# A GRU with a residual on one core: eight input units of the third step ahead of z's product in step 0, and one transfer moved

## Chip, cores and metric

The kernel runs on one core of a Trainium2 chip. The metric is the device time of one execution in microseconds (us). TensorE is called PE in the profile, its weight loads PEld; VectorE is DVE, ScalarE ACT, GpSimd POOL, and SP is the engine on whose queue most transfers are issued.

## What is computed

A GRU with 64 sequences, 128 steps, 512 inputs and 512 states, added to its own input. Every fourth step (but the last) the state goes through one more layer before the next step. Cut to what matters:

```
def step(h, inp):
    x_t, prop = inp
    comb = concatenate([x_t, h])
    z = sigmoid(comb @ Wz + bz)
    r = sigmoid(comb @ Wr + br)
    h_cand = tanh(concatenate([x_t, r * h]) @ Wh + bh)
    h_new = (1 - z) * h + z * h_cand
    h_next = where(prop, tanh(h_new @ Wp + bp), h_new)
    return h_next, h_new

return x + all h_new
```

All data are 32-bit floats. The upper 512 rows of each weight matrix meet x, the lower 512 the state.

## The kernel before

**Layout.** The 512 states stand as two halves (S = 2) of N = 256 columns, the 64 sequences of each half in 64 of the 128 partitions. A product over 512 rows has four blocks of 128 rows (k = 0 to 3, taken in ORDER = 0, 2, 1, 3). One *unit* is one block for one gate: `product` (L234) issues it for both halves, and the trace shows 4 matmuls of 128x256 for it (all on L225).

**State products and input products.** The weights for the state are in `wh[0..2]` (r, z, candidate), those for x in `wx`. A step needs the state products in order: r, then z, then the candidate with r * h. The input products don't depend on the state. They are kept as a list of units in `queue`; `fill(n)` (L416) issues the next n of them, so that they stand between the state products and give PE work while the other engines compute. When the last unit of a list has gone, `read_out()` (L423) issues the copies that bring its result, with the bias, from PSUM to the tile `cp` (L435 for r and z, L440 for the candidate; DVE). For steps 0 to 3 the units are plain (`plain`, L427: 12 units a step; for the third step in the order r, z, candidate, for the fourth block by block). From the fifth step on four steps at a time go through fewer products at the price of sums of weights and inputs (`batch`); the sums of weights are made once, in the first steps: `sum_outer` (L319 to L321, DVE, into the tiles `tw`), `sum_outer_1` (L325, DVE, in place), `sum_inner` and `sum_inner_1` (L328 to L330, L333, on POOL, a few on DVE).

**Order.** The schedule is written by hand: each engine runs its instructions in the order of the program text. PE, DVE, ACT and POOL each go through theirs one by one, with semaphores between the engines.

**Transposes.** A product takes its left operand transposed. `turn` (L241) does this for one half of the columns: four PE transposes (L248) and a copy out of PSUM (L239) by DVE or ACT. `turn_x(t)` turns x of step t (8 transposes, 2 copies), which the plain units of that step need. From the fifth step on x arrives by another route: small transfers `xs` (L157) and DVE transposes (`join_x`, L281).

**Step 0**, in the order of the text: r's four units (L728), then `turn_x(2)` (L732); r's sigmoid (L751) and rh = r * h (L752); three units of z (L762), rh's transposes (L766), z's fourth unit (L770); z and 1 - z (L775, L776), keep = (1 - z) * h (L777, DVE); `sum_outer` (L789) and `sum_inner` of one product (L791, POOL); `fill(12)` (L797), which are the 12 plain units of the third step; `turn_x(3)` (L799); the candidate's four units; then the copies of the third step's result, the tanh (L808, ACT), its product with z (L809) and the sum with keep (L814), both DVE, once for each half of the columns; `fill(5)` of the fourth step's units, the transposes of the new h's first half, one unit, those of its second half, six units; then `sum_outer_1` and `sum_inner_1` on DVE, and the first transposes of the `xs` route.

**Transfers at the start.** They are issued on SP one after the other: x of the first two steps, the weights for x (r, z, candidate), the weights for the state r, then x of the third and fourth step in two transfers, the weights for the state z and the candidate, sixteen `xs` transfers, the weights of the additional layer, its bias, and x of the next four steps.

Of the kernel before, what the change touches and what calls it, by code (L numbers as in the profile page):

```python
# [17 lines left out]
def kernel(  # L18
# [41 lines left out]
    R, Z, H_ = range(3)  # L60
# [32 lines left out]
    def load_x(tile_, t0, n, j=0):  # L93
        for s in range(S):
            nc.sync.dma_start(
                out=tile_[s * B : (s + 1) * B, j : j + n, :], in_=x[:, t0 : t0 + n, ts(s, N)]
            )

    def load_w(wt, w, k0, k1, eng):
        eng.dma_start(  # L100
            out=wt[:, k0:k1, :],
            in_=w[k0 * P : k1 * P, :].rearrange("(k p) n -> p k n", p=P),
        )

    ORDER = [s * C + c for c in range(C) for s in range(S)]
    xr = {}
# [33 lines left out]
    for i in range(3):  # L140
        for k in (0, 2):
            load_w(wh[i], gates_in[i][D:, :], k, k + 2, nc.sync)
        if i == 0:
            load_x(xr[0], 2, 2, 2)

    dummy = const.tile([1, 1], F32, name="dummy")
    nc.scalar.activation(dummy, ones[:, 0:1], AF.Sigmoid)
# [74 lines left out]
    def products(ps, lhs, rhs, start=False):  # L222

        for s in range(S):
            nc.tensor.matmul(  # L225
                ps[s * B : (s + 1) * B],
                lhsT=lhs,
                rhs=rhs(s),
                start=start,
                stop=True,  # L230
                skip_group_check=True,
            )

    def product(ps, lT, w, k, start=False):  # L234
        s0, c0 = divmod(k, C)
        products(ps, lT[:, c0, ts(s0, B)], lambda s: w[:, k, ts(s, N)], start)
# [4 lines left out]
    def turn(src, dst, c, name, eng):  # L241


        pt = turn_ps[c][:, :P].bitcast(BF16).rearrange("p (w n) -> p w n", w=2)
        for s in range(S):
            words = src[:, c * P + s * B : c * P + (s + 1) * B].bitcast(BF16)
            for w in range(2):
                nc.tensor.transpose(  # L248
                    pt[s * B : (s + 1) * B, w, :],
                    words.rearrange("p (n w) -> p w n", w=2)[:, w, :],  # L250
                    ident16,
                )
        copy(
            eng,
            dst[:, c, :].bitcast(U16).rearrange("p (n w) -> p n w", w=2),
            pt.bitcast(U16).rearrange("p w n -> p n w"),
        )
# [7 lines left out]
    def new_xT(g):  # L265
        if g not in xT:
            xT[g] = xtp.tile([P, Q4, C, P], F32, tag="xT", name=f"xT_{g}")

    def turn_x(t, eng=nc.scalar):
        g, i = divmod(t, Q4)  # L270
        new_xT(g)
        src = xr[g]
        for c in range(C):
            turn(src[:, i, :], xT[g][:, i], c, f"xT_{t}", eng)
# [141 lines left out]
    def fill(n):  # L416
        for _ in range(min(n, len(queue))):
            unit, end = queue.pop(0)
            unit()
            if end is not None:  # L420
                pending.append(end)
# [5 lines left out]
    def plain(t):  # L427

        first, second = scratch[:2] if t % 2 == 0 else scratch[2:]
        regions = (first[:, :N], first[:, N:], second[:, :N])  # L430
        g, i = divmod(t, Q4)

        def end():
            new_cp(t // 2)
            nc.vector.tensor_add(  # L435
                G[t][:, :, 0:2, :],
                first.rearrange("p (g c n) -> p c g n", g=2, c=C),
                bias[:, :, 0:2, :],
            )
            nc.vector.tensor_add(G[t][:, :, 2, :], cut(second[:, :N]), bias[:, :, 2, :])  # L440


        order = [(e, k) for e in range(3) for k in ORDER]
        if t == Q4 - 1:
            order = [(e, k) for k in ORDER for e in range(3)]
        units = [
            lambda e=e, k=k: product(
                regions[e], xT[g][:, i], wx[:, :, e, :], k, k == ORDER[0] and e != Z
            )
            for e, k in order  # L450
        ]
        return [(u, None) for u in units[:-1]] + [(units[-1], end)]
# [113 lines left out]
    def batches(g):  # L566

        if g * Q4 >= T:
            return []
        ms = [(g, i) for i in (1, 2, 6, 5, 7, 3, 4)]  # L570
        if g + 1 < LAST:
            ms += [(g + 1, i) for i in (1, 6, 2, 5, 3, 7, 4)]
        return sum((batch((g, n), ms[2 * n : 2 * n + 2]) for n in range(7) if 2 * n < len(ms)), [])
# [103 lines left out]
    for t in range(T):  # L677
# [6 lines left out]
        places = PLACES[u]  # L684
        if t == 0:
            queue.extend(plain(2) + plain(3))
            places = (12, 12)
        elif t == 1:
            queue.extend(batch((1, 0), [(1, 1), (1, 2)]))
            places = (8, 6)  # L690
        elif t == 2:
            queue.extend(batch((1, 1), [(1, 10), (1, 11)]) + batch((1, 2), [(1, 8), (1, 9)]))
            places = (12, 8)
        elif t == 3:
            queue.extend(batches(FIRST))
            places = (8, 8, 6)
        elif u == 7:

            queue.extend(batches(even + 2))
        thin = t >= T - 9  # L700
        if thin:

            places, behind = TAIL[t - (T - 9)]
        if t == T - 10:
# [7 lines left out]
            places = (4, 5)  # L712
# [13 lines left out]


        for k in ORDER:  # L728
            product(slots[R], hT, wh[R], k)
        if t < 2:  # L730
            if t == 0:
                turn_x(2)  # L732
        if t == 1:
            for i in (5, 7):
                sum_inner(i, nc.gpsimd)
# [19 lines left out]
            seed(H_, t)  # L755
        join(0)

        if t in (2, 3):
            fill((16, 6)[t - 2])


        for k in ORDER[: 2 if thin else 3]:  # L762
# [194 lines left out]
```

## Time and profile before

| | us |
|---|---|
| median of 3 runs | 1329.04 |
| their range | 1328.59 to 1329.49 |
| the profiled execution | 1330.24 |
| its span, first to last instruction | 1328.5 |
| PE busy (share) | 1319.2 (99%) |
| DVE, ACT, POOL busy | 750.8, 554.4, 881.5 |
| mean granted clock of PE | 0.999 |
| start of z's product, step 0 | 22.78 |
| start of the candidate's product, step 0 | 31.18 |

How to read it: a timeline line has the start from the beginning of the span, the time from the first start to the last end of the merged instructions, the engine, the source line, the operation, what it writes and reads, how many, and in brackets how long the engine stood before it and what ended that. Matmuls overlap: 16 of them start 1.73 us apart from the next group although the line gives 1.90 us, so durations of PE are taken from start to start.

### The profile page before, as it was taken

What the parts mean: (1) busy time and instruction counts of PE and PEld (TensorE: products, weight loads), DVE (VectorE), ACT (ScalarE), POOL (GpSimd) and SP (SyncE); (2) the same over time, 40 slices, a digit from 0 to 9 for tenths busy, and PEclk for the clock granted to TensorE, in tenths of its full rate; (3) what the DMA queues carried; (4) which work ended last, traced back from release to release, by engine and by line L of the source; (5) the groups of instructions that cost most, each with busy time, mean ns of one, the idle gap of its engine ahead of it and who ended that gap; (6) DMA issues with size and microseconds to landing.
All of it is one profiled execution on the core that took longest, in us unless ns stands there. A gap on an engine that the chain in (4) does not pass through costs nothing.

```text
span 1328.5 us, 37727 instructions
## 1 busy us (share of the span) xinstructions
PE 1319.2 (99%) x15312; PEld 1117.0 (84%) x15312; DVE 750.8 (57%) x2000; ACT 554.4 (42%) x1733; POOL 881.5 (66%) x1032
## 2 busy tenths in 40 slices
PE   9999999999999999999999999999999999999998
PEld 5888888888888888888888888888888888888865
DVE  3655555555555555555555555555555555555544
ACT  1344444444444444444444444444444444444433
POOL 4876766766767577675777757676676676757530
PEclk9999999999999999999999999999999999999999
DMA  8421122121121221222111221212212112121030
GB/s 236 90 50 30 21 49 49 33 49 34 33 49 33 54 45 18 49 43 56 33 33 34 50 49 34 47 20 49 49 34 49 34 33 49 33 49 33 18 104 17
DMA packets 171438, 62.22 MB, mean 47 GB/s; under 512 B 133600, under 2 KB 166496, under 8 KB 171264
## 3 DMA queue, kind: packets, MB, share of 16 engines
q1 hardware_dynamic: 170880, 59.47, 20.8%
q8 instruction: 121, 1.98, 0.6%
q14 instruction: 53, 0.43, 0.1%
q10 hardware_dynamic: 224, 0.20, 0.1%
q0 software_dynamic: 160, 0.14, 0.0%
HBM read 43.00 MB, written 16.78 MB: 45 GB/s over the span
## 4 chain that ended last, share of the span: by engine, by line
PE 96%; SPq 1%; DMA 1%; DVE 0%; issue 0%; ACT 0%; DVEq 0%; ACTq 0%
PE rc L225 33%; PE zp L225 20%; PE scratch_q L225 11%; PE scratch_r L225 11%; PE scratch_x L225 11%; PE scratch_a L225 5%; PE turn L248 5%; DMA xr<-in_x_dram 1%; SPq L157 1%; SPq L100 0%; DMA bias<-in_L_cond_bp_dram 0%; DVE wx L333 0%; DVE turn L809 0%; SPq L115 0%; DVE xT L281 0%
## 5 line engine op out<-in xcount | busy, mean ns | idle before, releaser
L225 PE MATMUL rc<-wh,rhT 128*64 128x256 f32 x2048 | 246.0, 379 | 0.0
L580 POOL TENSOR_TENSOR cp<-mb,mb 128x768 f32<-128x768 f32 x75 | 136.3, 1818 | 107.4 <-ACT rc L410 47.5
L225 PE MATMUL zp<-wh,hT 128*64 128x256 f32 x1536 | 204.6, 379 | 0.0
L225 PEld LDWEIGHTS rc<-wh,rhT 128*64 128x64 f32 x2048 | 168.6, 137 | 40.1
L225 PE MATMUL rc<-wh,hT 128*64 128x256 f32 x1536 | 186.5, 383 | 0.4
L891 POOL TENSOR_TENSOR xr<-xr,h 128x256 f32<-128x256 f32 x127 | 92.7, 730 | 126.3 <-DVE h L814 126.3
L225 PEld LDWEIGHTS rc<-wh,hT 128*64 128x64 f32 x1536 | 122.3, 137 | 36.1 <-issue 10.1
L580 POOL TENSOR_TENSOR cp<-mb 128x768 f32<-128x768 f32 x47 | 85.3, 1815 | 94.7 <-DVE h L814 89.8
L225 PEld LDWEIGHTS zp<-wh,hT 128*64 128x64 f32 x1536 | 119.7, 137 | 24.7
L809 DVE TENSOR_TENSOR turn<-turn,z 128x128 f32<-128x128 f32 x256 | 75.4, 295 | 102.2 <-ACT turn L808 100.7
L239 DVE COPY rhT<-turn 128x256 uint16<-128x256 uint16 x256 | 97.6, 420 | 56.0 <-PE turn L248 51.6
L751 ACT ACTIVATE turn<-rc 128x128 f32<-128x128 f32 x256 | 55.3, 260 | 171.4 <-issue 113.8
L239 ACT COPY hT<-turn 128x256 uint16<-128x256 uint16 x127 | 47.3, 373 | 165.5 <-DVE hT L239 130.7
L548 DVE TENSOR_TENSOR mb<-scratch_r,cq 128x384 f32<-128x384 f32 (+1 forms) x107 | 59.3, 554 | 91.8 <-ACT cq L547 90.3
L580 POOL TENSOR_TENSOR mb<-mb,mb 128x768 f32<-128x768 f32 x58 | 105.4, 1817 | 8.5 <-DVE mb L550 8.5
L541 DVE TENSOR_TENSOR cx<-scratch_r,cx 128x384 f32<-128x384 f32 (+1 forms) x107 | 59.3, 554 | 88.0 <-ACT cx L539 88.0
L775 ACT ACTIVATE z<-zp 128x256 f32<-128x256 f32 x128 | 49.2, 384 | 136.7 <-PE zp L225 136.7
L410 ACT COPY rc<-cp 128x256 f32<-128x256 f32 x256 | 96.4, 377 | 18.3 <-DVE cp L435 4.6
L808 ACT ACTIVATE turn<-rc 128x128 f32<-128x128 f32 x256 | 55.2, 260 | 112.8 <-PE rc L225 111.7
L814 DVE TENSOR_TENSOR h<-turn,keep 128x128 f32<-128x128 f32 x254 | 74.1, 292 | 15.2
L248 PEld LDWEIGHTS <-h 128*64 128x64 bf16 x1016 | 68.1, 110 | 12.2 <-DVE h L814 6.5
L248 PE MATMUL turn<-ident,h 128*64 128x128 bf16 x1016 | 77.8, 220 | 0.3 <-DVE h L814 0.3
(165 smaller groups left out, 2931.7 us busy)
## 6 DMA issues: line engine op xcount, KB each, us to landing
xs<-in_x_dram SPq DMA_DIRECT2D x248, 64.0 KB, 2.8
xr<-in_x_dram SPq DMA_DIRECT2D x62, 256.0 KB, 4.1
out_dram<-xr SPq DMA_DIRECT2D x62, 256.0 KB, 3.3
wx<-in_L_cond_Wr_dram SPq DMA_DIRECT2D x7, 256.0 KB, 4.5
wx<-in_L_cond_Wz_dram SPq DMA_DIRECT2D x2, 512.0 KB, 6.4
wx<-in_L_cond_Wh_dram SPq DMA_DIRECT2D x2, 512.0 KB, 9.5
wh<-in_L_cond_Wr_dram SPq DMA_DIRECT2D x2, 512.0 KB, 12.7
wh<-in_L_cond_Wz_dram SPq DMA_DIRECT2D x2, 512.0 KB, 13.0
```

What stands on the lines that cost most here:

```text
L225: nc.tensor.matmul(ps[s * B : (s + 1) * B], lhsT=lhs, rhs=rhs(s), start=start, stop=True, skip_group_check=True,)
L239: (eng.copy if eng is nc.scalar else eng.tensor_copy)(dst, src)
L248: nc.tensor.transpose(pt[s * B : (s + 1) * B, w, :], words.rearrange("p (n w) -> p w n", w=2)[:, w, :], ident16,)
L410: nc.scalar.copy(cut(slots[i]), G[t][:, :, i, :])
L541: nc.vector.tensor_add(T2[n][:, :nm], r_ps[:, :nm], T2[n][:, :nm])
L548: nc.vector.tensor_add(blocks()[:, :nm, 0, 1], r_ps[:, :nm], q2[:, :nm])
L580: nc.gpsimd.tensor_add(dst, a, b)
L751: nc.scalar.activation(act_ps[c], slots[R][:, ts(c, P)], AF.Sigmoid)
L808: nc.scalar.activation(pc, slots[H_][:, ts(c, P)], AF.Tanh)
L809: nc.vector.tensor_mul(pc, pc, z[:, ts(c, P)])
L814: nc.vector.tensor_add(h_new[:, ts(c, P)], pc, keep[:, ts(c, P)])
L891: nc.gpsimd.tensor_add(xr[g][:, j, :], xr[g][:, j, :], h_new)
```

## The change

x of the third and of the fourth step no longer come together behind r's state weights: the third's comes there, the fourth's behind z's state weights, each in two transfers of half the bytes. `turn_x(2)` goes in front of r's last unit. Eight of the third step's twelve plain units (r's four and z's four) are issued in front of z's state product, and four behind it. Line numbers of the changed kernel are one smaller from there on.

```
     for i in range(3):
         for k in (0, 2):
             load_w(wh[i], gates_in[i][D:, :], k, k + 2, nc.sync)
-        if i == 0:
-            load_x(xr[0], 2, 2, 2)
+        if i < H_:
+            load_x(xr[0], 2 + i, 1, 2 + i)
...
         if t == 0:
             queue.extend(plain(2) + plain(3))
-            places = (12, 12)
+            places = (4, 12)
...
         for k in ORDER:
+            if t == 0 and k == ORDER[3]:
+                turn_x(2)
             product(slots[R], hT, wh[R], k)
-        if t < 2:
-            if t == 0:
-                turn_x(2)
...
-        if t in (2, 3):
-            fill((16, 6)[t - 2])
+        if t in (0, 2, 3):
+            fill((8, 0, 16, 6)[t])
```

## The prediction

> **What bounds the kernel now.** First the page's share of busy time per engine, then the waits of PE, then the timelines of PE, DVE and POOL over the first 45 us: the change touches step 0 alone.
>
> ```profile
> PE 1319.2 (99%) x15312; PEld 1117.0 (84%) x15312; DVE 750.8 (57%) x2000; ACT 554.4 (42%) x1733; POOL 881.5 (66%) x1032
> PE zp L225 <- DMA wh<-in_L_cond_Wz_dram: 1.4, 2, 0.8
> ```
>
> PE works nearly all the time, so whatever delays PE in step 0 is carried to the end. All named waits of PE add up to 3.8 us in the whole run; the largest of them, 1.4 us in two pieces, is z's product waiting for its state weights. That is the wait the change works on. PE's timeline there (start, us, operation, count, idle before):
>
> ```profile
> 20.43 1.51 PE L225 MATMUL rc<-wh,hT_init 128*64 128x256 f32 x12 [0.38 <-DMA wh<-in_L_cond_Wr_dram]
> 21.78 0.41 PE L248 MATMUL turn<-ident,xr 128*64 128x128 bf16 x8
> 22.78 0.65 PE L225 MATMUL zp<-wh,hT_init 128*64 128x256 f32 x4 [0.60 <-DMA wh<-in_L_cond_Wz_dram]
> 24.21 1.08 PE L225 MATMUL zp<-wh,hT_init 128*64 128x256 f32 x8 [0.78 <-DMA wh<-in_L_cond_Wz_dram]
> 25.12 0.39 PE L248 MATMUL turn<-ident,rh 128*64 128x128 bf16 x8
> 25.35 0.60 PE L225 MATMUL zp<-wh,hT_init 128*64 128x256 f32 x4
> 25.78 3.62 PE L225 MATMUL scratch_q<-wx,xT 128*64 128x256 f32 x32
> 29.23 1.90 PE L225 MATMUL scratch_r<-wx,xT 128*64 128x256 f32 x16
> 30.96 0.39 PE L248 MATMUL turn<-ident,xr 128*64 128x128 bf16 x8
> 31.18 1.90 PE L225 MATMUL rc<-wh,rhT 128*64 128x256 f32 x16
> ...
> 35.07 0.28 PE L248 MATMUL turn<-ident,h 128*64 128x128 bf16 x4
> ...
> 41.61 0.51 PE L248 MATMUL turn<-ident,rh 128*64 128x128 bf16 x8
> ```
>
> From start to start a unit (4 matmuls) takes 0.43 us (16 take 1.73), eight transposes 0.22. The eight units that move are the row at 25.78: 3.45 us of work without any need of z's weights.
>
> Whether PE may use the time it wins is decided by DVE, which is in order and has no gap from z onward:
>
> ```profile
> 26.69 0.42 DVE L777 TENSOR_TENSOR keep<-zp,h_init 128x256 f32<-128x256 f32 x1 [0.48 <-ACT zp L776]
> 27.03 0.95 DVE L319 TENSOR_TENSOR tw<-wx 128x768 f32<-128x768 f32 x1
> ...
> 31.86 0.96 DVE L321 TENSOR_TENSOR tw<-wx,tw 128x768 f32<-128x768 f32 x1
> 32.74 0.69 DVE L435 TENSOR_TENSOR cp<-scratch_q,bias 128x512 f32<-128x512 f32 x1
> 33.34 0.41 DVE L440 TENSOR_TENSOR cp<-scratch_r,bias 128x256 f32<-128x256 f32 x1
> 33.67 0.29 DVE L809 TENSOR_TENSOR turn<-turn,z 128x128 f32<-128x128 f32 x1
> ...
> 35.74 2.62 DVE L325 TENSOR_TENSOR wx<-wx 128x768 f32<-128x768 f32 x2
> ```
> ```profile
> 35.80 1.76 POOL L333 TENSOR_TENSOR tw<-tw 128x384 f32<-128x384 f32 x1
> ```
>
> Between keep (which needs z) and the first product of the new h (L809) stand six sums of weights (L319 to L321, twice) and two copies, 6.98 us from start to start. The tanh is there by 33.45 (ACT 33.19 + 0.26), so L809 at 33.67 already waits for DVE, not for PE. The first half of h is done at 34.28, 0.8 us before PE turns it at 35.07: this is all the cover there is.
>
> **The change, part by part.**
>
> *x of the third step first (L728 to L732).* The 8 transposes stand in front of r's last unit. Eight matmuls after 20.43 end at 21.30. x of that step must have landed: before, two transfers of 128 KB landed at 21.21 and 21.6, behind r's weights at 20.4; now each has half the bytes, so about 21.0 (half of the 1.2 us). Cover 0.3 us; I take no wait; if it landed at 21.6 as before, everything below is 0.3 later. Then r's last unit, 21.52 to 21.95. ACT copies the transposes 0.33 us after their start (21.78 to 22.11 before), 0.37 us for the first: xT at 22.0, the eight units from 22.07. r's sigmoid comes 0.4 us earlier than at 22.64; nobody gains, since rh is wanted only behind z.
>
> *Eight units in front of z (L758).* 22.07 + 3.45 = 25.53. z's weights landed at 22.7 and 24.15, and come some 0.5 us earlier with 128 KB fewer in front (768 KB took 2.3 us): both waits go. z: 12 matmuls 1.30, rh's transposes 0.23, last unit 0.43: **z ends at 27.49 instead of 25.78, 1.71 later**. Then the four units left (1.73), x of the fourth step (0.22), and the candidate's product from 29.44 instead of 31.18: **PE is 1.74 us early** here. This is the gain, and it equals the two waits counted from issue to issue.
>
> *What is late next.* keep follows z: 26.69 + 1.71 = 28.40. POOL is idle from 26.1 until the second L320, so the six sums take as long as before, and L809 moves to 35.38, h's first half to 35.99. PE, through with the candidate at 31.17 and with its five units of the fourth step at 33.33, **stands 2.7 us and turns h at 36.02 instead of 35.07: 0.95 late**. The 1.74 are lost and 0.95 on top (1.71 less the cover, with 0.03 for the handover).
>
> *DVE behind that.* The copy of hT moves from 35.40 to 36.45, since L814's second half ends only at 36.52; the two L325 from 35.74 to 36.79. There POOL counts. The two L325 took 0.948 and 1.757 us, POOL's L333 1.756 against 1.007 for the same form later: operations of both that read SBUF twice wait for each other. POOL's chain (released by L320) moves by 1.71, L330 to 36.55-37.55, L333 behind it. Now the first L325 meets L330. If the engines take turns: L325 to 38.35 (0.8 after being let in, as in the 1.757), POOL to 39.2, second L325 to 40.0, instead of 38.36: 1.65 late. If POOL goes twice running: 40.2, 1.85 late. If the first L325 isn't held: 39.35, 1.0 late. I take turns, the way the row at 35.80 shows. The rest of DVE's line (L333, two transposes, two copies, rh at 41.29) has no gap and moves along: rh at 42.95, PE turns it at 43.27 instead of 41.61. PE's own line gives z's three units ending at 42.29, so it waits again, 1.0 us. **Sum +1.66 us, between +1.0 and +1.85.** Behind this POOL's sums and PE's batches hang on the same DVE transposes and shift together; the only later waits of PE are 0.2 and 0.3 us, nothing that could take the delay back.
>
> *SP.* One issue pair more. Each issue waits for the landing of the one eight before it (the second H load went at 16.36, when the load eight before landed at 16.3). x of the fourth step takes the slots at 13.09 and 16.36, the candidate's weights go at 18.84 and 20.4 (landings of r's), the xs loads behind x's landing near 21. By bytes the weights land at 25.6 and 26.9 as before, as the DMA engines are full until 24; by issue-to-landing (10.6 to 12.5) at up to 31.3. The candidate asks from 29.44, but its tanh is not used before 35.38: even 31.3 is hidden. Fourth x: wanted at 29.2, there about 24.2. The xs loads were done near 31 for a transpose at 39.69; a microsecond more is hidden. Cost 0.
>
> *The clock.* PE's granted clock is 1.00 in every stretch, but the longest idle in this trace is 1.20 us, and I foresee 2.7. The Trainium skill (TensorE: Matmul & The Clock Gate, Part 1) says the clock halves after an idle window of about 3.4 us. By that rule 2.7 us should still pass, though the window runs free; a window at half speed would lose about 1.7 us (an estimate from the page), and no row here shows it. The sum goes without it: whatever slows PE behind that stand has 1.0 us of cover in the second wait.
>
> **Rivals.**
> 1. *The waits go and the gain stays*: -1.74, **1327.3**. For it: the 1.74 at 29.44 is sure. Against: it needs h to be no later, and keep, six sums and L809 stand in one line on DVE. Chance 0.10.
> 2. *Neutral*: DVE's sums or the L325 pair go quicker than shown, and the cover takes most of it, **1329.0** to 1330.0. Chance 0.10.
> 3. *Slower by over 0.2%*: x of the third step lands late. It stands in front of r's last unit, so each microsecond past 21.30 delays xT, the eight units, z, keep and DVE's line one for one on top of 1.66. From a landing at 22.3 on the loss passes 2.66 us: **1331.7 and more**, about 1332.0. Against: r's weights landed at 20.4 and only 128 KB follow. Chance 0.10.
> 4. *It does not do what it says* is out: the built program has 32 matmuls of the third step in front of z's, and DVE, ACT and POOL keep their order.
>
> **Numbers.** The profiled execution took 1330.24 us for a span of 1328.5; with 1.66 it would be 1331.9. The median shown is 1.2 lower; the same shift gives **1330.7** (chance 0.70, 1330.0 to 1331.2). The range leaves out rival 1 and the far end of rival 3: 1328.6 to 1332.2. The bound for faster and slower is 0.2%, 2.66 us, about what a measurement of this kernel tells from no change. Faster by more would take almost all of PE's waits: 0.02, out of rival 1. Slower: rival 3 and 0.04 of the forecast's upper end, 0.14. Within: 0.84.
>
> **What would show it.** Right: no idle in front of zp in step 0; z's sigmoid near 27.7; L319 near 28.7; an idle of PE of some 2.7 us before turn<-ident,h put down to DVE L814's line; one of about 1 us before rh's transposes of step 1; one long L325 more. Wrong: keep near 26.7, so that h is not late; or x's transposes waiting for a DMA; or a granted clock under 1.00 behind 36 us.

## The result, and the profile after

| | before | changed |
|---|---|---|
| median of 22 runs each, us | 1329.22 | 1331.61 |
| range, us | 1327.96 to 1330.80 | 1331.12 to 1331.77 |
| profiled execution, its span, us | 1330.24, 1328.5 | 1331.56, 1329.7 |

The ratio is 1.0017, with a 95% interval of 1.0011 to 1.0023: about 2.3 us slower. This lies within the whole range of the prediction (1328.6 to 1332.2) and on the side it gave, but 0.9 us above its forecast of 1330.7 and 0.4 us above the upper end of that forecast's own band (1330.0 to 1331.2).

The page's line of busy times and PE's waits in the changed kernel:

```profile
PE 1320.1 (99%) x15312; PEld 1118.3 (84%) x15312; DVE 752.0 (57%) x2000; ACT 555.0 (42%) x1733; POOL 880.0 (66%) x1032
```
```profile
PE turn L248 <- DVE h L813: 2.8, 2, 2.6
PE rc L213 <- DVE zeros L73: 1.2, 1, 1.2
```

z no longer waits for its weights; the wait is gone from the list. In its place PE waits once for 2.6 us for DVE's h (the 0.3 us beside it were there before, at the end of the run). PE's timeline shows both:

```profile
18.88 1.47 PE L225 MATMUL rc<-wh,hT_init 128*64 128x256 f32 x12
20.18 0.39 PE L248 MATMUL turn<-ident,xr 128*64 128x128 bf16 x8
20.40 0.60 PE L225 MATMUL rc<-wh,hT_init 128*64 128x256 f32 x4
20.93 3.67 PE L225 MATMUL scratch_q<-wx,xT 128*64 128x256 f32 x32
24.43 1.47 PE L225 MATMUL zp<-wh,hT_init 128*64 128x256 f32 x12
25.73 0.39 PE L248 MATMUL turn<-ident,rh 128*64 128x128 bf16 x8
...
28.34 1.90 PE L225 MATMUL rc<-wh,rhT 128*64 128x256 f32 x16
...
34.94 0.31 PE L248 MATMUL turn<-ident,h 128*64 128x128 bf16 x4 [2.55 <-DVE h L813]
...
39.90 1.90 PE L225 MATMUL rc<-wh,hT 128*64 128x256 f32 x16
41.63 1.46 PE L225 MATMUL zp<-wh,hT 128*64 128x256 f32 x12
42.92 0.39 PE L248 MATMUL turn<-ident,rh 128*64 128x128 bf16 x8
```

r's product, the eight units and z follow each other without a wait that the view names. Behind the stand, the row at 34.94 to the row at 39.90 is one set of four transposes, one unit, another set and six units, 3.25 us of work by the rows of before (35.07 to 38.32); here it takes 4.96. The windows of PE in this execution (stretch, its length, busy time and count, granted clock, DMA share, GB/s) tell why:

```profile
32.50:34.90 2.40, 0.00 (x0) 1.00 0.86 216
34.90:35.20 0.30, 0.26 (x6) 1.00 0.92 307
35.20:35.40 0.20, 0.20 (x6) 0.60 0.71 276
35.40:38.40 3.00, 3.00 (x20) 0.50 1.08 322
38.40:38.80 0.40, 0.40 (x4) 0.69 1.14 241
38.80:39.20 0.40, 0.40 (x6) 1.00 0.91 177
```

The granted clock falls to a half just after PE has begun again. By the two mixed rows it is halved for 0.16 + 3.00 + 0.25 = 3.41 us, and PE loses half of that, 1.7 us. This is one profile, but hardly one execution alone: 1.7 us of 1329.7 take 0.0013 from the mean granted clock, and of the 22 runs 7 show 0.998, 15 show 0.999 and none 1.000, while 7 of 11 runs each of after_busy2 and six_ahead (below), whose profiles have no fall, show 1.000. DVE's timeline and POOL's row:

```profile
27.29 0.42 DVE L776 TENSOR_TENSOR keep<-zp,h_init 128x256 f32<-128x256 f32 x1 [0.48 <-ACT zp L775]
27.64 0.95 DVE L319 TENSOR_TENSOR tw<-wx 128x768 f32<-128x768 f32 x1
...
34.27 0.29 DVE L808 TENSOR_TENSOR turn<-turn,z 128x128 f32<-128x128 f32 x1
...
35.67 3.24 DVE L325 TENSOR_TENSOR wx<-wx 128x768 f32<-128x768 f32 x2
...
42.19 0.49 DVE L751 TENSOR_TENSOR rh<-turn,h 128x128 f32<-128x128 f32 x2 [0.28 <-ACT turn L750]
```
```profile
36.38 1.72 POOL L333 TENSOR_TENSOR tw<-tw 128x384 f32<-128x384 f32 x1
```

From keep to the tanh's product there are 6.98 us, as before: DVE's line has moved as a whole.

### The profile page after: what moved, and what is told of

Same layout as the page of the kernel before. It is cut to its first block, busy times and chain, and to the rows that moved or that the text cites. A ratio compares the mean times of both kernels' runs of the same rounds, so it can differ in the third digit from the quotient of the medians.

```text
span 1329.7 us, 37732 instructions
## 1 busy us (share of the span) xinstructions
PE 1320.1 (99%) x15312; PEld 1118.3 (84%) x15312; DVE 752.0 (57%) x2000; ACT 555.0 (42%) x1733; POOL 880.0 (66%) x1032
## 4 chain that ended last, share of the span: by engine, by line
PE 97%; DMA 2%; SPq 1%; DVE 1%; issue 0%; ACT 0%; DVEq 0%; ACTq 0%
PE rc L225 33%; PE zp L225 21%; PE scratch_q L225 11%; PE scratch_x L225 11%; PE scratch_r L225 11%; PE scratch_a L225 6%; PE turn L248 5%; DMA wh<-in_L_cond_Wz_dram 1%; DMA wx<-in_L_cond_Wz_dram 1%; SPq L157 0%; DMA xs<-in_x_dram 0%; SPq L100 0%; DVE turn L808 0%; DVE tw L320 0%; DVE tw L319 0%
## 5 line engine op out<-in xcount | busy, mean ns | idle before, releaser
L808 DVE TENSOR_TENSOR turn<-turn,z 128x128 f32<-128x128 f32 x256 | 75.5, 295 | 101.6 <-ACT turn L807 100.1
L813 DVE TENSOR_TENSOR h<-turn,keep 128x128 f32<-128x128 f32 x254 | 74.1, 292 | 15.2
```

The lines of the kernel that those rows point to most:

```text
L808: nc.vector.tensor_mul(pc, pc, z[:, ts(c, P)])
L813: nc.vector.tensor_add(h_new[:, ts(c, P)], pc, keep[:, ts(c, P)])
```

## The experiments

Every execution begins with transfers whose landing differs. In the profile of before, r's second half held PE until 20.43; in later profiles it did not hold PE at all. A second profile of the kernel before is therefore the one to set beside the changed kernel's. What comes behind step 1 does not differ: from the start of rh's transposes of step 1 to the end of the span there are 1286.7 to 1287.0 us in each of the twelve profiles, so whatever a kernel gains or loses here is gained or lost before that point.

**before_again**: the kernel before, unchanged.

> The kernel before once more, for its profile alone. The profiled execution of before was 1.0 us slower than the median of its runs, and in the changed kernel's profile r's state weights landed 1.6 us earlier. Theory A: the landing differs from execution to execution; here r's second half lands between 18.7 and 20.4, z still waits 1.2 to 1.8 us in all, and rh's transposes of step 1 start between 40.3 and 41.6, earlier by as much as r's weights. Rival (the change itself brings r's weights earlier): r's second half lands at 20.4 again.

It took 1329.20 us. Two lines of PE:

```profile
22.96 1.08 PE L225 MATMUL zp<-wh,hT_init 128*64 128x256 f32 x8 [0.70 <-DMA wh<-in_L_cond_Wz_dram]
...
40.36 0.51 PE L248 MATMUL turn<-ident,rh 128*64 128x128 bf16 x8
```

r's product ran from 19.18 without a wait, z still waited 1.0 us in two pieces, and rh's transposes of step 1 came at 40.36 instead of 41.61. So the early landing is not the change's doing. The changed kernel's row at 42.92 stands 2.56 us behind this one; the two spans differ by 2.4 us and the medians by 2.39, so nearly the whole loss is there at this point.

**loads_alone**: only the transfers.

```
-        if i == 0:
-            load_x(xr[0], 2, 2, 2)
+        if i < H_:
+            load_x(xr[0], 2 + i, 1, 2 + i)
```

> The transfers as in the change, the order of PE's work as before. Theory A (z, and with it keep and DVE's six sums, is what h waits for; the loss is DVE's line starting later plus PE's halved clock after its stand): z's weights have 128 KB fewer in front and come about 0.4 us earlier, so z, keep and DVE's line move 0.4 us forward: 0.3 to 0.5 us below before. Rival B (the two more issues on SP and the later weights of the candidate are the loss): 1.5 to 2.4 us above before. Rival C (the halved clock alone is the loss): as before, no stand, no drop.

1329.00 against 1329.30 us, ratio 0.9995 (0.9986 to 1.0003). z waited once, for 0.57 us, in this profile. That the transfers did this is not shown: in the profile of before_split (below), with the transfers as before, z waited once for 0.30 us. The time does not part a gain of 0.4 from nothing, but a loss of 1.5 us or more from the transfers (B) is excluded.

**order_alone**: `turn_x(2)` and the eight units as in the change, the transfers as before.

> The transfers as before, the order of PE's work as in the change. Theory A: the loss stays, 2.3 to 2.9 us above before (x of the third step lands a few tenths later and may hold the transposes). Rival B: about before, 0 to 0.3. Rival C: like A, since the stand and the drop stay; this run does not part A from C.

1332.13 against 1329.30 us, ratio 1.0021 (1.0012 to 1.0030): the whole loss is in the order of PE's work. The transposes waited 0.18 us for x (landed in transfers of full size), PE stood 2.55 us ahead of h again, and the clock fell again (0.53 in 36 to 38 us):

```profile
35.55 0.31 PE L248 MATMUL turn<-ident,h 128*64 128x128 bf16 x4 [2.55 <-DVE h L813]
...
43.52 0.39 PE L248 MATMUL turn<-ident,rh 128*64 128x128 bf16 x8
```

**after_busy**: the changed kernel with matmuls of zeros to fill the stand.

```
+            for _ in range(40):
+                nc.tensor.matmul(turn_ps[1][0:B, P:N], lhsT=zeros[:, :B],
+                                 rhs=zeros[:, :P], start=True, stop=True)
```

> The changed kernel with 40 small matmuls of zeros into unused PSUM while PE would stand ahead of h's transposes in step 0; nothing reads them. Theory A: the clock stays at 1.00, PE reaches rh's transposes of step 1 before DVE does, and these start at about 42.1 by DVE's line instead of 42.9: 0.6 to 0.8 us below the changed kernel, 1.5 to 1.8 above before. Rival C (the clock is the whole loss): as before, within 0.3. Rival B: as the changed kernel, 2.3 above before.

1334.68 against 1329.30 us, ratio 1.0036 (1.0024 to 1.0049). It missed all three expectations and does not part them: the bank they write is the one in which DVE forms h, so they waited for DVE themselves, 3.08 us, and then stood in front of h's transposes. It does show the clock fall a third time.

**after_busy2**: the same idea with 22 matmuls of 256 columns into the unused half of the bank of the fourth step's units, where nothing has to be waited for.

> The changed kernel with 22 matmuls of zeros (256 columns, about 2.35 us at full clock) behind the five units of step 0, into the unused half of a PSUM bank which no other engine touches then; they add zeros, nothing reads them. In the run before this one the filling matmuls waited for DVE like the transposes themselves and came behind the stand. Theory A: PE stands under 0.6 us ahead of h, the clock stays at 1.00, r's product of step 1 starts near 38.2 instead of 39.9, and rh's transposes at about 42.1 (DVE's line) instead of 42.9: 0.5 to 0.9 us below the changed kernel, 1.4 to 1.9 above before. Rival C (the halved clock is the whole loss): as before, within 0.4 us. Rival D (the drop costs nothing, as I had it in the prediction): as the changed kernel, 2.2 to 2.9 above before.

1330.91 against 1328.94 us, ratio 1.0015 (1.0006 to 1.0024). PE and its windows:

```profile
32.41 2.57 PE L224 MATMUL scratch_x<-zeros 128*64 128x256 bf16 x22
35.13 0.31 PE L259 MATMUL turn<-ident,h 128*64 128x128 bf16 x4
...
38.40 1.90 PE L236 MATMUL rc<-wh,hT 128*64 128x256 f32 x16
...
42.36 0.51 PE L259 MATMUL turn<-ident,rh 128*64 128x128 bf16 x8 [0.77 <-DVE rh L762]
```
```profile
36.00:38.00 2.00, 2.00 (x22) 1.00 1.09 317
```

The clock stays at 1.00 and r's product of step 1 follows h's transposes after 3.27 us instead of 4.96. Now PE stands 0.77 us at rh, which it did not in the changed kernel. From h's transposes to rh's there are 7.23 us instead of 7.98: of the 1.7 us that the clock took, 0.75 came through and the rest, 0.96, was hidden behind DVE. The same stretch tells the two groups apart in the other profiles: 7.97 in order_alone, where the clock fell, 7.23 in four_ahead and six_ahead (below), where it did not. In the times, 1.97 above before beside the changed kernel's 2.39, the two are not told apart, and 1.97 lies just outside both what A (1.4 to 1.9) and what D (2.2 to 2.9) had expected; the 0.75, and with it the case against D (the fall costs nothing), rests on the traces. C (the clock is the whole loss) falls: with the clock kept, about 2 us remain.

**four_ahead** and **six_ahead**: four and six units in front of z instead of eight.

```
-            places = (4, 12)
+            places = (8, 12)
...
-            fill((8, 0, 16, 6)[t])
+            fill((4, 0, 16, 6)[t])
```

> The changed kernel with four units ahead of z instead of eight (and eight behind). Four units are 1.73 us, as long as the wait for z's weights. Theory A: z ends when it did before, DVE's line starts when it did before, PE comes 1.7 us early to h's transposes and stands there about 0.9 us, too short for the clock to drop: before, within 0.4 us, though both waits for weights are gone. Rival C (the clock alone): before or up to 1.7 below, since nothing drops. Rival B: 1.5 to 2.4 above before.

> The changed kernel with six units ahead of z (and six behind). z ends 0.87 us later than with four, DVE's line starts 0.87 later. Theory A: the stand ahead of h is about 1.7 us; by DVE's line alone 0.8 to 1.1 us above before; if the clock drops behind a stand of 1.7 us as well, the time comes to 1.2 to 2.0 above before. Rival C (no drop, no loss): as before, within 0.4. A loss that begins only with eight units would speak against DVE's line as the cause.

Four: 1329.44 against 1329.28 us, ratio 1.0002 (0.9992 to 1.0011). Six: 1330.31 against 1328.94 us, ratio 1.0010 (1.0001 to 1.0019). Two lines of each:

```profile
34.06 0.31 PE L248 MATMUL turn<-ident,h 128*64 128x128 bf16 x4 [0.82 <-DVE h L813]
...
41.29 0.51 PE L248 MATMUL turn<-ident,rh 128*64 128x128 bf16 x8 [0.77 <-DVE rh L751]
```
```profile
34.87 0.31 PE L248 MATMUL turn<-ident,h 128*64 128x128 bf16 x4 [1.68 <-DVE h L813]
...
42.10 0.50 PE L248 MATMUL turn<-ident,rh 128*64 128x128 bf16 x8 [0.77 <-DVE rh L751]
```

With four units, 1.73 us and so about as long as the two waits in the profile of before, both waits for z's weights are gone and nothing is won: PE stands 0.82 us at h and 0.77 at rh. Two units more make the stand at h 0.86 longer, and the time 1.2 us more between the two medians' differences from before. The clock stays at 1.00 in both, so it has no part in this rise; what the trace shows of it is DVE's line. That the loss begins before any drop of the clock speaks against C again.

**after_split, four_split, before_split**: three of the six sums moved from behind keep to behind rh, in the changed kernel, with four units, and in the kernel before.

```
-    def sum_outer():
-        for ka in range(S):
+    def sum_outer(kas=range(S)):
+        for ka in kas:
...
         join(0)
+        if t == 0:
+            sum_outer((0,))
...
-            sum_outer()
+            sum_outer((1,))
```

> The changed kernel with the first three of DVE's six sums of weights moved from behind keep to behind rh, where DVE has a gap of 4.2 us. Theory A: DVE reaches the tanh's product at about 31.3 instead of 34.3, PE no longer stands ahead of h, the clock stays: 0.8 to 1.4 us below before, 3.2 to 3.7 below the changed kernel. Rival B: still 1.5 to 2.4 above before. Rival C: no drop, so about before, within 0.3.

> Four units ahead of z and three of DVE's sums behind rh. Theory A: z ends as before, DVE's line behind keep is 2.9 us shorter, nothing of DVE is late and PE keeps its whole gain: 1.2 to 1.8 us below before. Rival B: above before by 1.5 or more. Rival C: as four_ahead.

> The kernel before with three of DVE's sums behind rh, nothing else. Theory A: PE's waits for z's weights stay, h was not late before, so only the 0.1 to 0.3 us at rh's transposes of step 1 can be won: 0 to 0.4 us below before. The gain of the split in the other kernels would then be that of the two edits together. If the split alone wins over 0.8 us, A is wrong on where before is bound.

| | us | before, us | ratio (95% interval) | PE stands at h, at rh |
|---|---|---|---|---|
| after_split | 1328.53 | 1329.30 | 0.9993 (0.9984 to 1.0002) | none, 0.67 |
| four_split | 1328.02 | 1329.28 | 0.9989 (0.9981 to 0.9998) | none, 0.35 |
| before_split | 1328.95 | 1329.28 | 0.9998 (0.9989 to 1.0007) | none, none named |

The changed kernel with the split is 3.2 us below the changed kernel by their differences from before, about as A (h comes late by DVE's line) had it; its 0.77 below before is a little less than the 0.8 to 1.4 expected, and its interval reaches 1.0. The split alone is 0.3 us below before, which is not told from nothing. Four units with the split are below both kernels, 0.9 us below the split alone and 1.4 below the four units alone. DVE's line of four_split shows what the split does and what it costs:

```profile
22.40 1.24 DVE L319 TENSOR_TENSOR tw<-wx 128x768 f32<-128x768 f32 x1
23.68 1.65 DVE L320 TENSOR_TENSOR tw<-tw,wx 128x768 f32<-128x768 f32 x1
25.36 1.65 DVE L321 TENSOR_TENSOR tw<-wx,tw 128x768 f32<-128x768 f32 x1
...
27.59 0.41 DVE L778 TENSOR_TENSOR keep<-zp,h_init 128x256 f32<-128x256 f32 x1
...
31.70 0.29 DVE L810 TENSOR_TENSOR turn<-turn,z 128x128 f32<-128x128 f32 x1
```

Between keep and the tanh's product stand 4.11 us instead of 6.98, and h is there when PE comes. The first three sums cost 4.5 us in the gap instead of 2.9, because POOL's sums run beside them: in before_split, where POOL was through at 25.25, the third (from 26.09) took 0.96 again.

## Why the prediction was nearly right

The way that the delay takes (z, keep, DVE's line, h) was foreseen, and it gave the sign. The size was not: the sum allowed +1.0 to +1.85 us and 2.4 were measured, because one term stood at nothing. Of the signs named beforehand, no wait of zp, the stand ahead of h and the longer L325 came; the second stand of about 1 us did not; and one of the signs of being wrong came too, a granted clock under 1.00 behind 36 us.

- *x of the third step lands in time.* Right: its transposes had no wait, and 0.18 us with transfers of full size.
- *Eight units, then z, both waits go; z ends late.* Right: from the eight units to r * h's transposes and z's last unit every length is as worked out (3.50 for 3.46 us, z 1.96 for 1.96). All came about 1.1 us earlier than foretold (z's sigmoid at 26.60 instead of 27.7), since the first weights landed earlier in this execution.
- *h hangs on keep, six sums and two copies.* Right, and what decides the sign: 6.98 us from keep to L808, and a stand of 2.55 us, put down to L813 (the sum that makes h), where 2.7 were foreseen. four_ahead and the splits show it from both sides: the waits for weights can go without any gain, and the gain appears when DVE's line is shortened.
- *The two L325 and POOL take turns.* Right: 1.572 and 1.748 us instead of 0.948 and 1.757. The pair took 3.24 us (the row at 35.67), where the working gave 3.21.
- *The clock.* Here the prediction failed: "The sum goes without it: whatever slows PE behind that stand has 1.0 us of cover in the second wait." The stand was long enough for the clock to fall, in three kernels of three with a stand over 2.5 us. It took 1.7 us from PE, more than the cover. 0.75 us came through by after_busy2. The cover itself was right, 0.96 of the 1.0; the failed step is that the fall was left out of the sum because 2.7 us "should still pass". With the 1.7 that the text itself gave as an estimate, 0.7 would have been left over behind that cover. The second stand of 1.0 us, which the text foretold, is absent in the changed kernel and there in after_busy2 (0.77).
- *The rule weighed there.* The Trainium skill (TensorE: Matmul & The Clock Gate, Part 1) gives about 3.4 us of idleness for the fall, and a window of the same length for the way back. The length at half clock agrees, 3.41 us here. The idleness does not: 2.55 us were enough. Why the clock falls after 2.55 us stays open.
- *The sum.* 1.66 us by DVE's line; after_busy2, which has that line without the fall of the clock, measured 1.97 (interval 0.8 to 3.2). With 0.75 for the clock it is 2.4, the measured difference of the medians. That it meets so well is in part luck. The 1.66 was worked out on one execution, in which z waited 1.38 us; z waited 1.0 us in before_again and 0.30 in before_split, whose PE does the same up to there, and the less z waits, the more eight units delay it. Between the profiles of before_again and after_busy2, rh's transposes are 2.00 us apart (40.36 and 42.36), not 1.66. Rival 3 (x late) did not happen, though the time, 1331.61, comes near its 1331.7; rival 1 (gain kept) needed another edit on DVE.

## What to carry to other kernels

A wait that is filled on the busiest engine is a gain only if nothing that hangs on the delayed result is already just in time: before moving work in front of z, follow z through the in-order engines to the next moment at which the busy engine needs them. Look at the wait in more than one execution, and fill it with as much work as it is long, not twice as much: beyond the wait, what is moved past a product delays it one for one (two units more than four, 0.86 us of work, made the stand 0.86 us longer). And a stand of TensorE can have a second price in the clock (here behind 2.55 us), which comes after the stand and looks like slow matmuls.

## What had not been expected of the hardware

- The granted clock fell to 0.50 behind a stand of 2.55 us (changed kernel, order_alone) and 3.08 us (after_busy), but not behind 1.68, 0.82 or 0.77 us. It fell only after PE had begun again, and not at a fixed distance: 0.3 us after it in the changed kernel (35.24), 0.56 in order_alone (36.11) and 1.2 in after_busy (37.25). It stayed down for 3.41 us in all three. These are single profiles, so what decides between 1.68 and 2.55 us is not shown.
- DVE sums of 768 elements with both inputs in SBUF took 0.95 us alone and up to 1.76 beside POOL sums. For the two L325 the prediction had reckoned with this; that the sums moved behind rh would meet POOL's had not been expected. POOL's own went from 1.00 to 1.60 in four_split.
- The candidate's weights, issued 4.2 and 2.4 us later than before (at 17.32 and 18.74), landed 6.9 us behind their issue instead of 10.6 to 12.5, and so not later than before (near 24.2 and 25.6 us instead of 25.6 and 26.9). One profile of each stands behind this, and r's weights came earlier in the changed kernel's too.
